# Moving head rows, chunk preparation and x1 statistics to other points of a step schedule

## The chip, the cores and the metric

One NeuronCore of a Trainium2 chip runs the whole program. The metric is the device time of one execution in microseconds. The five engines are called by the profile's names: PE is the matmul engine, DVE the vector engine, ACT the scalar engine, POOL the GpSimd engine, and SP the engine whose queue issues nearly all DMAs of the part that is changed.

## The reference

The input `r` is 8 sequences of 2048 points with 512 features. Two blocks follow each other, each with a layer norm in front, a layer norm behind, and a residual sum:

```python
def _L0_attn_ref(r, ...):                 # a state space layer
    ...
    h1 = jnp.fft.irfft(uf * Kf.T[None], n=nfft, axis=1)[:, :seq_len]
    y1 = h1 + D[0] * r
    return jax.nn.gelu(y1, approximate=False)

def _L0_ffn_ref(x, ...):                  # a gated recurrence over axis 0 (8 steps)
    def step(c, xt):
        ft = jax.nn.sigmoid(xt @ wf.T + c @ uf.T + bf)
        it = jax.nn.sigmoid(xt @ wi.T + c @ ui.T + bi)
        gt = jnp.tanh(xt @ wc.T + c @ uc.T + bc)
        return ft * c + it * gt, None
    c_final, _ = lax.scan(step, c0, x)
    return jnp.tanh(jnp.einsum('tbi,oi->tbo', x, wo) + c_final @ uo.T + bo)

x = L0_attn_r
x = x + _layernorm(_L0_attn_ref(_layernorm(x, axis=-1), ...), axis=-1)    # called x1 here
x = x + _layernorm(_L0_ffn_ref(_layernorm(x, axis=-1), ...), axis=-1)
```

The recurrence runs over the eight sequences: sequence index 0 to 7 is its time `t`, and each of the 2048 points is a row of its batch. So the output row of a point at any `t` needs the state after all eight steps.

## The kernel before, in words

**The first part** (up to about 690 us) computes the state space layer as a blocked convolution, group by group, and stores its result `y` to DRAM as `y_d`. Neither the diff nor anything in it touches this part.

**The second part** is the recurrence. The 2048 points are cut into four quarters `q` of 512 points, each of four chunks `cj` of 128. A step is one pair `(q, t)`; there are 32 steps, `n = 8 q + t`. The matrix products are done by a scheme with seven products in place of eight on 256-wide blocks, each in three fp16 pieces, so PE has many 128x256 matmuls (line 950).

A step is eight slots. Each holds one unit of PE's work: two units `z0`, `z1` (the output projection of x), and six gate units, called `g0` to `g5` here: input, candidate, forget gate for one half of the features, then the same for the other half. A unit is done in two pieces. `part_a` makes four products for a z unit and, for `t > 0`, eight for a gate unit; ACT (line 988) and DVE (lines 989 to 992) then add partial sums in PSUM. `part_b` makes the rest, and ACT evacuates: lines 1002 and 1003 (tile `zt`) for a z unit, line 1016 for a gate. The next unit's `part_a` lies between the two pieces of a unit. With `t > 0`, `part_b` of `z1` waits until after `part_a` of `g1`. PSUM has three `u` buffers for these units. The last gate of a half also makes the new state (`state`, lines 1036 to 1042) and its fp16 pieces `cf` (lines 1049 and 1051), which the next step's gates need.

**Points.** Everything else is hung on the points of this chain. Slot `s` has the points `2s` (after its `part_a`) and `2s + 1` (after the `part_b` that follows). A step therefore has the points 0 to 15, and 16 is point 0 of the next step. `put(functions, base, points)` appends one function to each point's list, and `go(p)` runs that list; a later `put` comes later in the list:

```python
put(turn(*steps[n + 1], i), b, ps[i])
...
part_a(key)
go(p)
...
finish(before, p + 1)        # part_b; the store of a z unit is put at its next point
go(p + 1)
```

In this part the order of PE, ACT, DVE, POOL and SP is the program's order. Each engine runs its own list in that order, so the first instruction that must wait holds up all behind it on its engine. What is hung on the points:

- `prep`: one chunk of x1 for two values of `t`: load `y` (SP, line 880), load `xr` (SP, 890), stat (DVE, 462 to 465), scale (POOL, 471 to 476), sum (ACT 903, POOL 904), store to `x1_d` (SP, 911; the DRAM tensor `x_d` in the profile). The tiles `y` and `xr` have one buffer each.
- `turn`: two chunks of x1 for the next step: load `xa` (SP, 925), stat, scale, norm (ACT, 936), split (PE transposes, 485, with ACT 489 and DVE 490 to 492), halves (`xf`: ACT 101 and DVE 102 in alternation). It runs twice in a step, `i = 0, 1`.
- `head`: one output row block of the quarter before (128 points at one `t`; 32 in a quarter, in the seven steps with `t > 0`: five in each of the first four, four in each of the last three). Load `zr` (SP, 1120; every eighth head also `ur`, 1118), sum (POOL, 1123), gate (ACT, 1126), stat, scale, load `x1r` (SP, 1136), out (ACT 1140, POOL 1141), store (SP, 1144). `zr` has four buffers, `x1r` two.
- `last`: in the step `t = 0` of a quarter, the part of the output that depends on the final state of the quarter before: four groups of 128x512 matmuls (450 to 452) in the same three `u` buffers, evacuated by ACT (1097) and summed by POOL (1100). It has a loaded `bo` in an `x1r` buffer, and its four `u_` tiles in `zr` buffers.
- the store of a z unit (SP, 1007 to 1009). The tile `zt` has one buffer: the next z unit's evacuation waits for that store.

After the last step comes `tail`: the 32 rows of the last quarter in 16 pairs. It loads `zz` (SP, 1157) and `xx` (SP, 1169), sums (DVE 1174), and stores (SP, 1190); the tiles are reused after nine pairs, so a later load of `xx` waits for an earlier pair's store.

Of the kernel before, what the change touches and what calls it, by code (L numbers as in the profile page):

```python
# [22 lines left out]
NB = 8  # L23
# [36 lines left out]
def s4_gated_block(ctx, tc, a, dbg=None):  # L60
# [54 lines left out]
    with ExitStack() as sctx:  # L115
        sp = sctx.enter_context(tc.tile_pool(name="setup", bufs=1, side="right"))
        ps = sctx.enter_context(tc.tile_pool(name="setup_ps", bufs=2, space=PSUM))
# [337 lines left out]
    def lnstat(src, tag):  # L455

        n = len(src)
        st = FE.tile([P, n, 6], F32, name="st" + tag)
        mv = FE.tile([P, n, 2], F32, name="mv" + tag, bufs=2)
        rs = FE.tile([P, n], F32, name="rs" + tag, bufs=2)  # L460
        for i, v in enumerate(src):
            V.bn_stats(st[:, i], v)  # L462
        for i in range(n):
            V.bn_aggr(mv[:, i], st[:, i])
        V.tensor_scalar(rs, mv[:, :, 1], EPS, None, ALU.add)  # L465
        return n, mv, rs, tag

    def lnscale(s_, neg=True):

        n, mv, rs, tag = s_  # L470
        Q.tensor_tensor(rs, rs, nhalf[:, 0:n], ALU.pow)  # L471
        mu = mv[:, :, 0]
        if neg:
            mu = FE.tile([P, n], F32, name="nm" + tag, bufs=2)
            Q.tensor_tensor(mu, mv[:, :, 0], rs, ALU.mult)
            Q.tensor_scalar(mu, mu, -1.0, None, ALU.mult)
        return [(mu[:, i : i + 1], rs[:, i : i + 1]) for i in range(n)]
# [102 lines left out]
    with ExitStack() as cctx:  # L580
# [220 lines left out]
        for g in range(NG):  # L801
# [17 lines left out]
            with tc.manual_schedule(engines=MAN if nxt else MAN | {mybir.EngineType.SP}):  # L819
# [18 lines left out]
                for s_ in range(NJ):  # L838
                    if s_ % 2 == 0 and s_:
                        conv_out(g, s_ // 2 - 1)  # L840
                    if nn:

                        d = ND1 if g == 1 else 0
# [71 lines left out]
    def turn(q, t, i):  # L915

        xa, s_ = [], []

        src = xa if q or t > 1 else [early["x1", i + 2 * h] for h in range(2)]

        def load():
            for h in range(2):
                x = FE.tile([P, H], F32, name="xa", bufs=2)
                if src is xa:
                    dma(out=x, in_=x1_d[QC * q + i + 2 * h, :, t])
                xa.append(x)

        def stat():
            s_.append(lnstat(src, "x"))

        def scale():
            s_.extend(lnscale(s_.pop()))

        def norm():
            for x, v, (nm, rs) in zip(xa, src, s_):
                S.activation(x, v, AF.Identity, scale=rs, bias=nm)

        def split_():
            pt = pq_.tile([P, 2, KT, P], F32, name="pt")
            xa[:] = [forms(q, t, i, xa, [pt[:, h] for h in range(2)])]  # L940

        return load, stat, scale, norm, split_, lambda: xa[0]()
# [168 lines left out]
    def head(q, cj, t):  # L1111

        c, s_ = QC * q + cj, {}

        def load():
            if c not in us_:
                us_[c] = FJ.tile([P, H], F32, name="ur", tag="wr")
                dma(out=us_[c], in_=u_d[c])
            s_["z"] = FT.tile([P, H], F32, name="zr", bufs=4)
            dma(out=s_["z"], in_=z_d[c, :, t])  # L1120

        def sum_():
            Q.tensor_tensor(s_["z"], s_["z"], us_[c], ALU.add)  # L1123

        def gate():
            S.activation(s_["z"], s_["z"], AF.Tanh, scale=1.0 / SW)

        def stat():
            s_["s"] = lnstat([s_["z"]], "h")

        def scale():
            s_["s"] = lnscale(s_["s"])[0]

        def load_x():
            s_["x"] = FT.tile([P, H], F32, name="x1r", bufs=2)
            dma(out=s_["x"], in_=x1_d[c, :, t])

        def out():
            nm, rs = s_["s"]
            S.activation(s_["z"], s_["z"], AF.Identity, scale=rs, bias=nm)  # L1140
            Q.tensor_tensor(s_["x"], s_["x"], s_["z"], ALU.add)  # L1141

        def store():
            dma(out=a["out"][c, :, t], in_=s_["x"])

        return load, sum_, gate, stat, scale, load_x, out, store
# [62 lines left out]
    def put(fs, base, ps):  # L1209
        for f, p in zip(fs, ps):  # L1210
            todo.setdefault(base + p, []).append(f)
# [5 lines left out]
    steps = [(q, t) for q in range(NQB) for t in range(NB)]  # L1217
    pairs = [(q, tp) for q in range(NQB) for tp in range(NB // 2)]
    chunks = [(g, cj) for g in range(1, len(pairs)) for cj in (0, 2, 1, 3)]
    at_ = lambda *p: [tuple(range(i, i + 6)) for i in p]  # L1220
    when = [(0, (0, 0, 3, 4, 5, 6)), (0, (0, 0, 5, 6, 7, 8)), (0, (9, 9, 11, 12, 13, 14))] + [(1, p) for p in at_(1, 6)]
    PA, PB = (5, 5, 7, 8, 10, 11), (12, 12, 16, 17, 19, 20)
    for n, (q, t) in enumerate(steps):

        if n > 1 and t:
            when += [(n, p) for p in (at_(5, 10, 15) if t in (2, 3) or n == 4 else at_(5, 10) if t == NB - 1 else (PA, PB))]
    end = last(NQB - 1)
    rows = [tail(NQB - 1, cj, tp, 4 * cj + tp) for cj in range(QC) for tp in range(NB // 2)]

# [5 lines left out]
    for n, (q, t) in enumerate(steps):  # L1235
        b = 16 * n
        if n + 1 < len(steps):
            ps = ((2, 5, 6, 7, 8, 9), (9, 10, 11, 12, 13, 14)) if n else ((0, 1, 2, 3, 5, 6), (5, 6, 7, 8, 9, 10))
            for i in range(2):
                put(turn(*steps[n + 1], i), b, ps[i])  # L1240
        if q and t == 0:
            put(last(q - 1), b, (-1, 4, 3, 5, 5, 7, 7, 9, 13, 14, 15))
        if n == len(steps) - 1:
            put(end[:2], b, (2, 3))
            for i in range(3):
                put(rows[i][:2], b, (8 + 2 * i, 9 + 2 * i))
        for (gp, cj), (n_, p) in zip(chunks, when):
            if n_ == n:
                put(prep(*pairs[gp], cj, (1, 0, 2)[cj] if n == 0 else 0), b, p)
        if q and t:  # L1250
            for i in range(5 if t < 5 else 4):
                r = 5 * t - 5 + i - max(t - 5, 0)
                put(head(q - 1, r // NB, r % NB), b, [1 + 3 * i + d for d in (0, 2, 4, 6, 8, 9, 10, 12)])
    with tc.manual_schedule(engines=MAN | {mybir.EngineType.SP}):
        before = None
        for n, (q, t) in enumerate(steps):
# [8 lines left out]
            for sl, key in enumerate(zs + gs if n else gs[:5] + zs + gs[5:]):  # L1265
                p = 16 * n + 2 * sl
# [85 lines left out]
```

## Time and profile before

| | us |
|---|---|
| median of 3 runs (2898.7 to 2905.06) | 2899.93 |
| the profiled execution's own time | 2900.85 |
| its span | 2899.1 |
| PE busy | 2588.2 (89%) |
| DVE busy | 2102.1 (73%) |
| ACT busy | 1478.8 (51%) |
| POOL busy | 1185.9 (41%) |
| DMA, mean | 156 GB/s |

The times of the profile count from the start of the span. The profiled execution is 1.75 us longer than its span and 0.92 us longer than the median. In the timeline a line gives start, duration, engine, source line, operation, tiles and count; the bracket behind it is the idle time of that engine before it, and what ended it. "SPq" is SP's queue of DMA issues.

### The profile page before, as it was taken

The page shows a single profiled execution, that of the slowest core. Times are in us where ns is not written, and L with a number is a line of the kernel's source. Part 1 is how long each engine was busy: PE and PEld are TensorE (multiplying, and loading weights), DVE is VectorE, ACT ScalarE, POOL GpSimd, SP SyncE. Part 2 cuts the span into 40 slices and gives each one's busy share as a digit, 9 for nine tenths or more (in the row PEclk, how much of TensorE's full clock was granted, in tenths as well). Part 3 has the DMA queues.
Part 4 walks back from the last instruction along what each step waited for, and adds up shares of the span by engine and source line. Part 5 has one row for each costly group of instructions (what it writes and reads, how often), then busy time and mean ns, then how long its engine had stood idle before and what let it go on. Part 6 is the DMA issues. An engine that isn't in the chain of part 4 may idle for free.

```text
span 2899.1 us, 60027 instructions
## 1 busy us (share of the span) xinstructions
PE 2588.2 (89%) x23940; PEld 2255.6 (78%) x23940; DVE 2102.1 (73%) x4248; ACT 1478.8 (51%) x3091; POOL 1185.9 (41%) x1496
## 2 busy tenths in 40 slices
PE   4678888885999999999999998999999899999990
PEld 3367777774888888878888886888888788888870
DVE  7868877747666776667777776777777677777757
ACT  8956666643434443445555454454545445444435
POOL 5757667714112221114454341345443324443227
PEclk8789999987999999999999999999999999999995
DMA  6867878787423433324664443355554334532338
GB/s 233 304 209 241 259 251 260 241 248 189 154 66 95 114 84 96 91 88 124 160 172 135 121 124 99 101 159 167 145 149 120 117 89 147 151 117 89 95 119 298
DMA packets 521937, 451.10 MB, mean 156 GB/s; under 512 B 289974, under 2 KB 401080, under 8 KB 516664
## 3 DMA queue, kind: packets, MB, share of 16 engines
q1 hardware_dynamic: 521224, 446.74, 52.0%
q8 instruction: 187, 3.06, 0.4%
q14 instruction: 94, 0.77, 0.1%
q10 hardware_dynamic: 432, 0.52, 0.1%
HBM read 295.41 MB, written 151.78 MB: 154 GB/s over the span
## 4 chain that ended last, share of the span: by engine, by line
PE 50%; DVE 13%; ACT 5%; DMA 4%; issue 2%; POOL 1%; SPq 0%; POOLq 0%; DVEq 0%; ACTq 0%
PE u L950 47%; PE pt L485 1%; DVE u L992 1%; DMA z_d<-zc 1%; DVE cf L1051 1%; ACT xf L101 1%; DVE cd L1037 1%; DMA y<-y_d 1%; ACT gate L1016 1%; DVE sty L462 1%; DVE gate L1036 1%; ACT y L903 1%; DMA z_d<-zt 1%; DVE u2p L989 1%; DVE sth L462 1%
## 5 line engine op out<-in xcount | busy, mean ns | idle before, releaser
L950 PEld LDWEIGHTS <-w 128*128 128x128 f16 x15120 | 1482.0, 98 | 216.0 <-issue 30.8
L950 PE MATMUL u<-xf,w 128*128 128x256 f16 x8064 | 945.4, 274 | 32.1 <-ACT zt L1003 15.4
L950 PE MATMUL u<-cf,w 128*128 128x256 f16 x7056 | 825.9, 273 | 1.5 <-DVE cf L1051 1.5
L950 PE MATMUL u<-w,xf 128*128 128x256 f16 x2688 | 314.2, 275 | 15.2 <-DVE u L992 5.2
L1141 POOL TENSOR_TENSOR x1r<-x1r,zr 128x512 f32<-128x512 f32 x96 | 133.6, 1392 | 453.8 <-ACT zr L1140 344.6
L988 ACT ACTIVATE u2p<-u 128x256 f32<-128x256 f32 x256 | 96.7, 378 | 433.9 <-PE u L950 433.7
L1016 ACT ACTIVATE gate<-u,bias 128x512 f32<-128x512 f32 (+1 forms) x384 | 200.6, 574 | 217.9 <-PE u L950 217.8
L904 POOL TENSOR_TENSOR xr<-y,xr 128x512 f32<-128x512 f32 x120 | 160.1, 1354 | 351.7 <-ACT y L903 351.5
L950 PEld LDWEIGHTS <-xf 128*128 128x128 f16 x2688 | 264.6, 99 | 49.8 <-issue 10.7
L989 DVE TENSOR_TENSOR u2p<-u2p,u 128x256 f32<-128x256 f32 x256 | 106.8, 417 | 258.7 <-ACT u2p L988 256.8
L992 DVE TENSOR_TENSOR u<-u,u2p 128x512 f32<-128x512 f32 x256 | 179.0, 699 | 8.8
L647 POOL TENSOR_TENSOR u<-xg,u 128x512 f16<-128x512 f32 x104 | 128.7, 1242 | 124.6 <-ACT u L645 124.6
L641 POOL TENSOR_TENSOR xg<-xg,mu 128x512 f32<-128x512 f32 x112 | 162.7, 1459 | 9.7 <-DMA xg<-in_xr 9.7
L471 POOL TENSOR_TENSOR rsy<-rsy,nhalf 128x2 f32<-128x2 f32 (+1 forms) x68 | 49.4, 726 | 284.3 <-DVE rsy L465 272.4
L102 DVE TENSOR_TENSOR x<-pxt,x 128x256 f16<-128x256 f32 x240 | 100.1, 418 | 70.7 <-ACT x L101 69.5
L1021 DVE SCALAR_TENSOR_TENSOR gate<-gate,gate 128x1024 f32<-128x1024 f32 x64 | 88.2, 1378 | 83.2 <-ACT gate L1016 82.8
L462 DVE BATCH_NORM_STATS2 sty<-y 128x6 f32<-128x512 f32 x120 | 76.8, 682 | 86.9 <-DMA y<-y_d 86.9
L1123 POOL TENSOR_TENSOR zr<-zr,ur 128x512 f32<-128x512 f32 x96 | 125.7, 1309 | 20.9 <-DMA zr<-z_d 16.4
L101 ACT ACTIVATE x<-pxt 128x256 f16<-128x256 f32 x240 | 91.2, 381 | 79.6 <-PE pxt L667 73.4
L452 PE MATMUL pyt<-u,t 128*128 128x128 f16 (+2 forms) x544 | 124.8, 229 | 5.5 <-POOL u L623 5.5
L450 PE MATMUL pyt<-u,t 128*128 128x128 f16 (+2 forms) x544 | 121.8, 224 | 6.2 <-ACT y L746 3.1
L101 ACT ACTIVATE xf<-pt 128x512 f16<-128x512 f32 x124 | 60.7, 490 | 128.6 <-DVE xf L102 116.5
(371 smaller groups left out, 5352.2 us busy)
## 6 DMA issues: line engine op xcount, KB each, us to landing
xs<-in_rr SPq DMA_DIRECT2D x32, 1024.0 KB, 7.1
t<-kpad SPq DMA_DIRECT2D x32, 1024.0 KB, 5.5
y_d<-y SPq DMA_DIRECT2D x30, 1024.0 KB, 7.5
xr<-in_r SPq DMA_DIRECT2D x60, 512.0 KB, 5.6
xa<-x_d SPq DMA_DIRECT2D x120, 256.0 KB, 4.1
y<-y_d SPq DMA_DIRECT2D x59, 512.0 KB, 5.8
x_d<-xr SPq DMA_DIRECT2D x59, 512.0 KB, 3.2
xg<-in_xr SPq DMA_DIRECT2D x28, 1024.0 KB, 8.3
```

The lines of the kernel that those rows point to most:

```text
L101: S.activation(hi, src, AF.Copy)
L452: T.matmul(out, lhsT=w(0), rhs=x(1), start=False, stop=stop)
L462: V.bn_stats(st[:, i], v)
L641: Q.tensor_tensor(xg, xg, bc(mu1), ALU.subtract)
L647: (V if g == 2 else Q).tensor_tensor(u[:, js, 1], xg, u[:, js, 0], ALU.subtract)
L904: Q.tensor_tensor(xv, yv, xv, ALU.add)
L950: T.matmul(u[:, d], lhsT=w(f, b, i == 1, k), rhs=x(f, b, i == 2, k), start=opens and bank not in seen, stop=stop and j == len(n) - 1, skip ...
L989: V.tensor_tensor(u2, u2, u[:, UY], ALU.add)
L992: V.tensor_tensor(u[:, 2:4], u[:, 2:4], u2[:, None].to_broadcast([P, 2, BP]), ALU.add)
L1016: act = lambda o, s_, b: S.activation(o, s_, AF.Tanh, scale=gsc[kind], bias=b)
L1123: Q.tensor_tensor(s_["z"], s_["z"], us_[c], ALU.add)
L1141: Q.tensor_tensor(s_["x"], s_["x"], s_["z"], ALU.add)
```

## The change

Nothing is computed differently, and no instruction is added or taken away; functions are put at other points.

```diff
-    at_ = lambda *p: [tuple(range(i, i + 6)) for i in p]
-    when = [(0, (0, 0, 3, 4, 5, 6)), (0, (0, 0, 5, 6, 7, 8)), (0, (9, 9, 11, 12, 13, 14))] + [(1, p) for p in at_(1, 6)]
-    PA, PB = (5, 5, 7, 8, 10, 11), (12, 12, 16, 17, 19, 20)
+    two = (2, 2, 5, 6, 7, 8), (8, 8, 10, 11, 12, 13)
+    three = (-2, -2, 4, 5, 6, 7), (6, 7, 9, 9, 10, 11), (10, 11, 15, 16, 17, 18)
+    when = [(0, (0, 0, 3, 4, 5, 6)), (0, (0, 0, 5, 6, 7, 8)), (0, (9, 9, 11, 12, 13, 14))] + [(1, p) for p in two]
     for n, (q, t) in enumerate(steps):
 
         if n > 1 and t:
-            when += [(n, p) for p in (at_(5, 10, 15) if t in (2, 3) or n == 4 else at_(5, 10) if t == NB - 1 else (PA, PB))]
+            when += [(n, p) for p in (three if t in (2, 4) or n == 6 else two)]
...
-            ps = ((2, 5, 6, 7, 8, 9), (9, 10, 11, 12, 13, 14)) if n else ((0, 1, 2, 3, 5, 6), (5, 6, 7, 8, 9, 10))
+            ps = ((2, 5, 6, 7, 8, 9), (9, 10, 11, 12, 13, 14)) if t else ((2, 4, 5, 6, 7, 8), (7, 8, 9, 10, 11, 13)) if n else ((0, 1, 2, 3, 5, 6), (5, 6, 7, 8, 9, 10))
...
         if q and t:
             for i in range(5 if t < 5 else 4):
                 r = 5 * t - 5 + i - max(t - 5, 0)
-                put(head(q - 1, r // NB, r % NB), b, [1 + 3 * i + d for d in (0, 2, 4, 6, 8, 9, 10, 12)])
+                put(head(q - 1, r // NB, r % NB), b, [2 * i + d for d in (0, 2, 3, 5, 6, 5, 7, 8)])
```

The points of a `prep` stand in the order load, load_x, stat, scale, sum, store; of a `turn` load, stat, scale, norm, split, halves; of a `head` load, sum, gate, stat, scale, load_x, out, store. So a head started every three points and lived for twelve; it starts every two and lives for eight. The last store of a step's heads moves from point 25 (five heads) or 22 (four) to 16 or 14. `prep` no longer reaches past point 13, but for the third of the steps with three, which ends at 18; those are the steps `t = 2, 4` (and `t = 6` in the first quarter), where they were `t = 2, 3` (and 4 in the first). `turn` moves in the steps `t = 0` of the last three quarters alone.

## The prediction

> **What bounds the kernel now.** The page first. PE is busy nearly the whole span, so what can be won is PE's idle time, and the chain behind the last matmul.
>
> ```profile
> PE 2588.2 (89%) x23940; PEld 2255.6 (78%) x23940; DVE 2102.1 (73%) x4248; ACT 1478.8 (51%) x3091; POOL 1185.9 (41%) x1496
> ```
>
> Next, stretches of the second part: a step without heads, then the starts of the second and third quarters (steps t = 0), then a step with heads (t = 3, last quarter). Columns: stretch, length, busy time and count of PE, PEld, DVE, ACT, POOL, the granted clock, DMA.
>
> ```profile
> 1142.00:1208.00 66.00, 66.00 (x607) 59.34 (x606) 44.75 (x88) 28.79 (x59) 15.72 (x21) 1.00 0.30 81
> 1208.00:1270.00 62.00, 54.02 (x411) 40.64 (x409) 40.62 (x79) 27.13 (x57) 8.98 (x11) 0.97 0.26 86
> 1732.00:1799.00 67.00, 57.50 (x430) 42.58 (x429) 40.37 (x79) 30.23 (x61) 16.33 (x20) 0.95 0.28 91
> 2468.00:2536.00 68.00, 64.57 (x590) 57.58 (x588) 51.94 (x107) 33.84 (x66) 33.20 (x46) 1.00 0.60 159
> ```
>
> A step without heads is PE alone: 66 us, no idle time, 66/607 = 0.109 us a matmul. A step with heads idles 3.4 us, a quarter's start 8.0 or 9.5. Third, what PE waited for between 1200 and 2810 us (in total, times, longest):
>
> ```profile
> PE u L950 <- ACT zt L1003: 15.4, 19, 2.2
> PE u L450 <- ACT zt L1003: 7.9, 3, 3.6
> PE u L451 <- DVE cf L1051: 4.9, 5, 2.2
> PE pt L485 <- ACT xa L936: 3.5, 3, 1.2
> PE u L950 <- ACT u__16431 L1097: 3.0, 1, 3.0
> ```
>
> With its other lines it sums to 50.2 us. Placed by the timeline's brackets, 17.4 us in 22 waits lie in the first third of steps t >= 2 and 33.0 us in the three quarter starts (7.8, 12.5, 12.7). A wait costs 0.16 us more than its bracket, since a matmul takes 0.273 us and the next starts after 0.109.
>
> Fourth, the timeline behind such a wait (q = 1, t = 4; the step starts at 1463.3):
>
> ```profile
> 1479.85 0.80 ACT L1140 ACTIVATE zr<-zr,nmh,rsh 128x512 f32<-128x512 f32 x1
> 1480.55 0.61 ACT L1126 ACTIVATE zr<-zr 128x512 f32<-128x512 f32 x1
> 1482.24 2.78 PE L950 MATMUL u<-xf,w 128*128 128x256 f16 x24 [0.86 <-ACT zt L1003]
> 1487.51 0.32 SPq L911 DMA_DIRECT2D x_d<-xr  x1
> 1489.66 0.38 SPq L1007 DMA_DIRECT2D z_d<-zt  x1
> 1494.22 0.38 ACT L1002 ACTIVATE zt<-u 128x256 f32<-128x256 f32 x1 [4.58 <-DMA z_d<-zt]
> 1495.15 2.78 PE L950 MATMUL u<-xf,w 128*128 128x256 f16 x24 [1.61 <-ACT zt L1003]
> ```
>
> Two ACT instructions of heads stand between the `cf` pieces and `zt` of z0, and PE loses 0.86. Then z0's store stands in SP's queue behind a chunk's store, which waited for POOL; the second `zt` waits for that store, and PE for `zt`. At a quarter's start the same happens, worse (1749 to 1757): a head's store, bo's load behind it, and z0's store only at 1752.19.
>
> Last, the end of step t = 0 (1263) and the tail:
>
> ```profile
> 1261.88 0.38 ACT L101 ACTIVATE xf<-pt 128x256 f16<-128x256 f32 x1 [2.23 <-DVE xf L102]
> 1263.11 0.59 ACT L1097 ACTIVATE u__16431<-u 128x512 f32<-128x512 f32 x1
> 1263.75 4.41 PE L950 MATMUL u<-w,xf 128*128 128x256 f16 x24 [3.04 <-ACT u__16431 L1097]
> 2823.44 0.34 SPq L1144 DMA_DIRECT2D out<-x1r  x1
> 2823.87 0.38 SPq L1157 DMA_DIRECT2D zz<-z_d  x1
> 2845.42 0.32 SPq L1169 DMA_DIRECT2D xx<-x_d  x1
> ```
>
> The halves of turn 1 (point 14) hold ACT while DVE is at its `u2p` chain; `u_` comes after them, and PE lacks its buffer. In the tail SP stands before the last head's store until 2823.44; the pairs' loads come after it.
>
> **Part 1, starts of steps, about 15 us gained.** The 22 waits cost 17.4 + 22 x 0.16 = 20.9 us. A head now ends at point 16, so between points 0 and 2 neither ACT nor DVE has head work; ACT gets 1.41 us (0.80 + 0.61) back ahead of `zt`, more than the 0.86 lost, and the 0.85 and 0.35 to 0.41 waits for DVE and `cf` go with the head and chunk statistics (0.68 to 1.9 us each) leaving the edge. z0's store then goes out when `zt` is written, some 14 us into the step, and lands 4.1 us later (median of that DMA); the second `zt` is due at 23.6 (24 + 36 + 24 + 18 + 48 + 48 + 18 matmuls x 0.109).
>
> The exception is the step after one with three chunks (t = 3 and 5, six times). The third chunk's store is at point 2, followed there by the loads of the next chunk, and `xr` has one buffer: its load waits for that store to land. By the rows: `cf` done at 13 us into the step, `y` on ACT to 14.6 (1.51), POOL sum to 16.5 (2.5), store, landing 3.2 after issue, so `xr` near 20, two head loads, z0's store at 21.4, landed near 26. The second `zt` ends near 27.3, PE wants the buffer at 27.5. The step's second head queues behind the same load: its `zr` lands at 24.6, and ACT's gate waits for it and POOL's sum, to the same 26. So between 0 and 3.5 us each; I take 1, six times 6 us. 20.9 - 6 = 15. In the first quarter (no heads; steps 3, 5, 7 now follow three chunks) PE shows no wait between 760 and 1208; bound 0 to 3 us, I take 0.
>
> **Part 2, edge of quarters, about 15 us.** At the second quarter's start, where no heads precede it, the waits up to the second `zt` are 0.34 + 1.01; at the third 2.21 + 0.34 + 0.16 + 3.28, at the fourth 0.42 + 1.63 + 0.34 + 0.16 + 3.63. The new heads end at point 14 there, so both become like the first: 4.6 and 4.8 us of waits, 0.8 us of their 0.16s, and the half clock behind the long ones: after 3.28, eighteen 512-wide matmuls at 0.43 instead of 0.215 for most of their run, 3.1 us by the starts; 1.7 at the fourth. Sum 15.
>
> **Part 3, turn in t = 0, about 4 us, of both signs.** Slots here are short (24 and 18 matmuls). Turn 1's halves go from point 14 to 13, where 18 matmuls of `last` and a `part_a` (6.5 us) cover them: the 3.04 goes, with 1.8 us of half clock in two of three cases, and the 1.17 for `xa`, as the norm is two points earlier. But turn 0's halves go from 9 to 8, in front of g1's evacuation. Queued behind them on ACT is line 1016, and the `part_a` of g3 waits for it. Step by step: ACT `u2p` 0.38 after g2's end, `xf` 0.59, DVE's chain of four (2.06) and its 0.68, ACT 0.38 + 1.05, then gate 0.50 + 1.05: 6.0 us after g2's `part_a`, where PE is free after 1.97. A wait of 4.0 in place of 1.14, and half clock behind it, 0 to 3.1, I take 1.8. The 1.14 before `last`'s third group falls to 0.45, covered by the transposes (0.87) now ahead of it. Before, with the 0.16s: 3 x 7.1 + 3.6 = 25.0. After: 3 x (0.45 + 0.2 + 4.0 + 0.48 + 1.8) = 20.8. If the cover at point 13 fails, 12 us are lost instead.
>
> [...]
>
> **Part 4, tail, about 5 us.** The last two heads' stores (2818.22, 2823.44) leave SP; they went out after the last matmul. The loads of pairs 3 to 8 went out from 2823.9 to 2833.9 and the first pair's store, in that crowd, took 10 us to free `xx` (2835.23 to 2845.42); each later load waits 5.7 to 6.2 us for the next store, down to 2875.3. Earlier loads let that store land in the usual 5.6 and leave at 2833.9. That is 5 to 6 us earlier through the chain; DVE, which waits there (2.73, 1.71, 3.76), would follow. Bounds 0 and 7.
>
> **What costs nothing.** Per head: four SP DMAs, POOL 1.27 + 1.0 + 1.27, ACT 0.62 + 0.80, DVE 1.0, all moved, none new. In mid-step a gate's slot is 9.2 us of PE and its chain needs 2.5, so 6.7 us of delay on ACT and DVE together is covered; the densest point (7: norm 1.51, `y` 1.51, out 0.80, gate 0.62) makes 4.4. `zr` is reused by the fourth next head, whose load (point 8) follows the out at 7. `x1r`'s load waits for a store one point before, landing in 2.6 us (median), while a point is 4. Behind it wait prep's and turn's loads; turn 1's `xa` would issue at 40 us into the step, land at 44, and DVE reaches it near 46.5.
>
> **Sum.** 15 + 15 + 4 + 5 = 39 us. 2900.85 - 39 = 2861.9 for the profiled execution, which stood 0.9 above the median; I predict 2862.
>
> **Rivals.**
> *A. The new landing wait decides.* `xr`'s wait for the chunk store puts z0's store later than counted, at the upper bound of 3.5 us in six steps (-15). Alone that leaves 24 us, 2877. With part 3 at a worse end (half clock of 3.1 us after all three waits: -4; the cover at point 13 failing: -12) and a tail that gives nothing (-5, as DMA moves 257 GB/s there already) it leaves 7 to 15, about 2889. For it: SP shows 354 us of waiting at that chunk store. Against: a wait of SP costs only what stands behind it.
> *B. Slower.* SP's queue clogs at points 8 and 9: chunk store, its landing, head store, its landing, and behind them turn 1's `xa`. DVE, in order, stands before `xa`'s statistics and holds the gates' `u2p` chain. DVE covers about 6 us there; beyond it every step with heads pays, 21 of them. From 39/21 = 1.9 us a step it eats the gain; at 3 us, 63 - 39 = +24, 2924. For it: the store's longest landing is 7.4 us. Against: 2.6 is the median.
> *C. Nothing*: the waits only change names, 2896 to 2904.
>
> **How the numbers follow.** Forecast (gains of 25 to 55) 0.60, A (gains of 7 to 25) 0.21, B 0.13, C 0.06. A measurement can tell 0.2%, about 5.8 us, so the forecast and A make faster 0.81, C same 0.06, B slower 0.13. The range goes from 2848 (the 6 us of part 1 not paid, and 8 of part 3's new wait hidden) to 2888 (through nearly all of A); B and C stay outside.
>
> **What would show it.** Right: waits of PE for `zt` in the matmuls of line 950 fall from 15.4 to below 7, and sit in steps t = 3 and 5; the 3.04 for line 1097 is gone; a wait for line 1016 of about 4 us appears in each t = 0; the tail's first `xx` reload is 5 us sooner after the last matmul. Wrong: new PE waits in mid-step, or DVE waiting for `xa<-x_d` in every step.

## The result, and the profile after

The changed kernel takes 3007.62 us (median of 4 runs, 3001.71 to 3011.18) against 2899.31 us for the kernel before beside it. The ratio is 1.0374, with an interval of 1.0354 to 1.0394: slower by 108 us, where 39 us of gain were forecast. The execution in its profile took 3006.43 us, its span 3004.6 us, so 105.5 us more than the span before.

The first view of the page, busy time by engine, answers to the first line shown of before:

```profile
PE 2621.0 (87%) x23940; PEld 2264.2 (75%) x23940; DVE 2118.7 (71%) x4248; ACT 1481.1 (49%) x3091; POOL 1176.5 (39%) x1496
```

The counts are the same. PE is busy 32.8 us longer for the same matmuls, so part of the loss is a lower clock (the mean granted clock is 0.957, 0.962 before), and the rest is idle time.

What PE waited for between 1200 and 2920 us (in total, times, longest):

```profile
PE u L950 <- DVE u L992: 63.1, 32, 3.9
PE u L950 <- ACT zt L1003: 17.1, 5, 4.4
PE u L950 <- ACT gate L1016: 16.6, 12, 3.9
PE pt L485 <- ACT xa L936: 14.9, 5, 4.4
...
PE u L450 <- ACT zt L1003: 3.0, 3, 1.0
PE u L950 <- DVE cf L1051: 3.0, 8, 0.9
```

The line on top is new: before, the wait for DVE's line 992 was one of 0.8 us. With all its lines this window's sum rises from 54.4 us in 48 waits to 123.7 in 74; between 705 and 1200 us it rises from 17.7 in 7 to 24.4 in 13. The last matmul starts at 2942.49 instead of 2829.69, 112.8 us later. Of that, 76.0 are these waits, and about 5 the 0.16 us that each of the 32 added waits costs beyond its bracket. The remaining 32 are put down to the lower clock behind the waits; the 32.8 us that PE is busy longer agree with it. From the last matmul to the end of the span it is 62.1 us instead of 69.4: the tail gives 7.3 back.

Line 992 is the end of DVE's partial sums of a unit. What made it late is in the groups of the page, which show what ended the idle time just before each group:

```profile
L490 DVE TENSOR_TENSOR ts<-pt,b 128x512 f32<-128x512 f32 x62 | 42.6, 687 | 237.7 <-ACT b L489 229.6
...
L1123 POOL TENSOR_TENSOR zr<-zr,ur 128x512 f32<-128x512 f32 x96 | 127.4, 1328 | 207.3 <-DMA zr<-z_d 202.7
...
L489 ACT ACTIVATE b<-pt 128x256 f32<-128x256 f32 x124 | 40.5, 380 | 261.3 <-DMA z_d<-zc 250.1
```

ACT, in order, stood 250 us in front of line 489 until a DMA out of `zc` had landed, and DVE behind it 230 us. Among ACT's waits between 1200 and 2920 us it is the largest:

```profile
ACT b L489 <- DMA z_d<-zc: 202.1, 20, 12.5
```

Before, the same wait was 39.7 us in 13, 5.5 at the longest, all of it in this window.

Line 489 belongs to `turn`'s split and has nothing to do with `zc`, but for the buffer. In the code the two tiles are declared with one tag, of one buffer:

```python
b1 = FJ.tile([P, 2, 2, P], F32, name="b1", tag="un")        # line 486, in turn's split
...
gates["z"] = FJ.tile([P, 2, BP], F32, name="zc", tag="un")  # line 980, the z units
```

`zc` is free when the store of `z1`, the second z unit of the step, has landed (line 1009). The timeline of one step (q = 1, t = 1, from point 7 on) follows it through:

```profile
1304.68 0.38 ACT L988 ACTIVATE u2p<-u 128x256 f32<-128x256 f32 x1 [0.15 <-PE u L950]
...
1305.21 0.32 SPq L911 DMA_DIRECT2D x_d<-xr  x1
1305.63 0.53 SPq L880 DMA_DIRECT2D y<-y_d  x1
1308.49 1.29 SPq L890 DMA_DIRECT2D xr<-in_r  x1
1309.88 0.42 SPq L1144 DMA_DIRECT2D out<-x1r  x1
1310.39 0.38 SPq L1120 DMA_DIRECT2D zr<-z_d  x1
1310.82 1.13 SPq L1007 DMA_DIRECT2D z_d<-zt  x1
...
1312.53 0.45 SPq L1009 DMA_DIRECT2D z_d<-zc  x1
...
1316.84 0.66 ACT L489 ACTIVATE b<-pt 128x256 f32<-128x256 f32 x2 [11.78 <-DMA z_d<-zc]
1317.53 0.69 DVE L490 TENSOR_TENSOR ts<-pt,b 128x512 f32<-128x512 f32 x1 [10.38 <-ACT b L489]
...
1326.60 2.14 PE L950 MATMUL u<-xf,w 128*128 128x256 f16 x18 [2.31 <-DVE u L992]
...
1339.06 3.79 PE L950 MATMUL u<-xf,w 128*128 128x256 f16 x18 [2.01 <-DVE u L992]
```

At point 8 SP's list is: the first chunk's store, the second chunk's `y` and `xr` loads, a head's store, a head's load, and only then `z1`'s store. `z1`'s last piece of `zt` was written at 1296.43, so its store was ready to go nearly 9 us before the chunk's store, on which SP stood for 16.3 us until POOL had the chunk's sum. The chunk's store goes out at 1305.21, just when ACT comes to line 489; `xr` has one buffer, so its load stands until that store has landed, at 1308.49. `z1`'s store leaves between 1310.82 and 1312.53 and lands at 1316.84, and ACT has stood still for 11.78 us. Behind line 489 on ACT are the evacuations of a gate (1016) and the halves, on DVE the split and two gates' `u2p` chains; by 1326.60 and again at 1339.06 PE has nothing left to run. With `z1`'s store put in front and nothing else moved (`z1_first` below), ACT stands 0.49 us in front of line 489 in this step, and PE has no wait in it.

### The profile page after: what moved, and what is told of

Its sections match the earlier page's. It is cut to its first block, busy times and chain, and to the rows that moved or that the text cites. A ratio compares the mean times of both kernels' runs of the same rounds, so it can differ in the third digit from the quotient of the medians.

```text
span 3004.6 us, 59995 instructions
## 1 busy us (share of the span) xinstructions
PE 2621.0 (87%) x23940; PEld 2264.2 (75%) x23940; DVE 2118.7 (71%) x4248; ACT 1481.1 (49%) x3091; POOL 1176.5 (39%) x1496
## 3 DMA queue, kind: packets, MB, share of 16 engines
q8 instruction: 187, 3.06, 0.4%
## 4 chain that ended last, share of the span: by engine, by line
PE 32%; DVE 21%; DMA 8%; ACT 5%; POOL 3%; issue 3%; SPq 3%; ACTq 0%; POOLq 0%; DVEq 0%
PE u L950 30%; DMA z_d<-zc 3%; DMA x_d<-xr 3%; POOL xr L904 2%; DVE cf L1051 2%; DVE cd L1037 2%; DVE gate L1036 2%; DVE xf L102 2%; ACT gate L1016 1%; ACT xf L101 1%; DVE u L992 1%; SPq L890 1%; DVE gate L1021 1%; DVE sth L462 1%; ACT xa L936 1%
## 5 line engine op out<-in xcount | busy, mean ns | idle before, releaser
L950 PE MATMUL u<-xf,w 128*128 128x256 f16 x8064 | 969.1, 278 | 116.5 <-DVE u L992 74.0
L1141 POOL TENSOR_TENSOR x1r<-x1r,zr 128x512 f32<-128x512 f32 x96 | 139.7, 1455 | 346.8 <-ACT zr L1140 341.7
L490 DVE TENSOR_TENSOR ts<-pt,b 128x512 f32<-128x512 f32 x62 | 42.6, 687 | 237.7 <-ACT b L489 229.6
L471 POOL TENSOR_TENSOR rsx<-rsx,nhalf 128x2 f32<-128x2 f32 (+1 forms) x66 | 55.2, 836 | 352.5 <-DVE rsx L465 352.5
L489 ACT ACTIVATE b<-pt 128x256 f32<-128x256 f32 x124 | 40.5, 380 | 261.3 <-DMA z_d<-zc 250.1
L452 PE MATMUL pyt<-u,t 128*128 128x128 f16 (+2 forms) x544 | 124.7, 229 | 5.0 <-POOL u L623 5.0
```

Of the source, the lines that this page charges most:

```text
L452: T.matmul(out, lhsT=w(0), rhs=x(1), start=False, stop=stop)
L950: T.matmul(u[:, d], lhsT=w(f, b, i == 1, k), rhs=x(f, b, i == 2, k), start=opens and bank not in seen, stop=stop and j == len(n) - 1, skip ...
```

## The experiments

Theory S, the store: the new `prep` points put a chunk's store, its landing and a load ahead of `z1`'s store, so that `zc`, and with it line 489, comes free too late. Its narrow form says that the landing wait of the second chunk's `xr` does it. Rival H, the heads: two points apart they crowd ACT, DVE and POOL. Short diffs are against the kernel before ("before +") or the changed one ("after +"); "..." stands for code left out. The kernel before ran beside each; its median lay between 2896.8 and 2900.5 us, so versions are compared by their ratio to it.

### Which of the three parts

`heads_only`: before + the new points of the heads.

```diff
-                put(head(q - 1, r // NB, r % NB), b, [1 + 3 * i + d for d in (0, 2, 4, 6, 8, 9, 10, 12)])
+                put(head(q - 1, r // NB, r % NB), b, [2 * i + d for d in (0, 2, 3, 5, 6, 5, 7, 8)])
```

> The kernel before with the new head points alone. Theory S (the store of z1, which frees the tile that zc and b1 share, stands too far back in SP's queue, and what puts it back is the chunk store and the load that waits for its landing, both new at point 8): the heads add only one store and one load ahead of it, and their work leaves the edges, so this is faster than before by 10 to 25 us, about 2880, and ACT waits for z_d<-zc under 60 us in total. Rival H (two x1r buffers at two-point spacing clog SP by themselves): slower by at least half of the 108 us, 2950 or more, with SP waiting for out<-x1r about 69 us as in the changed kernel.

Measured: 2895.68 us, 0.9985 (0.9976 to 0.9994), a gain of about 4 us. PE's waits, then ACT's:

```profile
PE u L950 <- DVE u L992: 18.1, 6, 3.4
...
PE u L950 <- ACT zt L1003: 2.4, 3, 1.9
```

```profile
ACT b L489 <- DMA z_d<-zc: 89.5, 20, 7.2
```

The starts of steps get what was forecast (15.4 us of waits for `zt` fall to 2.4), and the wait for `zc` takes it away again. H is out as the cause of the loss, since it expected 2950 or more. But S missed too: the gain is below the 10 to 25 us that it expected, and the wait for `zc` above its 60. With the new heads alone `z1`'s store is late too; `heads_turn_z` below shows what that was worth.

`prep_only`: before + the new `two`, `three` and `when`, heads and turn as before.

> The kernel before with the new chunk points alone. Theory S: slower by 50 to 110 us (2950 to 3010), since the chunk store, then a load that waits for its landing, stand ahead of z1's store at point 8; ACT waits for z_d<-zc over 150 us. Rival H: within 20 us of before.

Measured: 3054.93 us, 1.0534 (1.0519 to 1.0548): 155 us slower, beyond the range expected. PE waits 56.4 us in 33 for DVE's line 992, ACT 150.7 us for `zc`. The chunk points alone make the loss and more. Not all of it goes through `zc`: PE's waits for `zt` rise as well, to 32.7 us in 22, and those for `xa` to 24.1 in 8.

`turn_only`: before + the new `ps`.

> The kernel before with the new x1 points of the steps t = 0 alone. Both theories: a wait of about 3.9 us of PE for line 1016 in three places and the 3.04 us for line 1097 gone; by the prediction's part 3 a gain of about 4 us (2 to 8), since in the changed kernel the half clock behind the new wait is not seen everywhere.

Measured: 2891.48 us, 0.9963 (0.9949 to 0.9977), 11 us gained, more than expected. Heads and turn without the new chunk points (`heads_turn`, before + both):

> The kernel before with the new head points and the new turn points of t = 0, chunks as before. If the parts add: 2900 - 4.5 - 10 = 2886 (2880 to 2891).

Measured: 2883.10 us, 0.9948 (0.9936 to 0.9961). 0.0015 and 0.0037 add up to it: 15 us. Beside the new chunk points the same two are worth 0.0534 - 0.0374 = 0.016, 46 us, so the parts don't add: the new chunk points cost more beside the old heads than beside the new ones. Why was not traced.

### Which wait it is

`z1_first`: after + the store of `z1` first in its point's list.

```diff
-                if st_:
+                if st_ and key[2:] == ("z", 1):
+                    todo.setdefault(p + 1, []).insert(0, st_)
+                elif st_:
```

> The changed kernel, with the store of z1 put at the front of the list of its point 8 and not at its end; nothing else moves. Theory S: ACT's wait for z_d<-zc falls from 250 us to under 60 and 70 to 110 us come back, 2895 to 2935; the waits for zt in the steps t = 3 and 5 stay. Rival H: less than 30 us come back, 2975 or more, as heads and chunk loads stand as they did.

Measured: 2925.72 us, 1.0080 (1.0064 to 1.0096). One DMA group, ahead of the others at its point, brings back 0.0294, 85 of the 108 us. The wait for `zc` and PE's for line 992:

```profile
ACT b L489 <- DMA z_d<-zc: 50.5, 5, 11.0
```

```profile
PE u L950 <- DVE u L992: 13.3, 5, 3.5
```

Over the whole span ACT's wait for `zc` falls from 250.1 to 67.1 us, a little above the 60 expected; the five waits shown sit in steps with three chunks. For 85 of the 108 us S is shown. `two_gap` asks for the narrow form. After +:

```diff
-    two = (2, 2, 5, 6, 7, 8), (8, 8, 10, 11, 12, 13)
+    two = (2, 2, 5, 6, 7, 8), (9, 9, 11, 12, 13, 14)
```

> The changed kernel with the second chunk of a step with two a point later, (9, 9, 11, 12, 13, 14): at point 8 SP still has the first chunk's store ahead of z1's store, but no longer the load that waits for its landing. Theory S in its narrow form (the landing wait is what costs): ACT's waits of 12 us for z_d<-zc become 7 to 8 in these steps, and 40 to 75 us come back, 2930 to 2965. If the chunk store's own wait for POOL is what costs: under 25 us come back, 2980 or more.

Measured: 2944.63 us, 1.0162 (1.0146 to 1.0178): 0.0212, 61 us back. The second chunk's loads now stand behind `z1`'s store, not before it; the whole second chunk is a point later too, so the edit isn't the wait alone. In the steps with two chunks ACT's waits become 3.4 to 7.6 us, where they were 10.5 to 12.4; in the step shown 7.61, from 11.78. These 4.2 us are what the two loads took of SP there, 1305.63 to 1309.78: about 2.2 of them the landing wait, the rest the issue of the two loads. So over half of the loss goes with the two loads in front of `z1`'s store, but the narrow form, that it is the landing wait alone, is not shown. By the rows of this step, what `two_gap` leaves of the 85 is the other DMAs ahead of the store, its own issue and landing, which come too late once it stands behind the chunk's store, and the steps with three chunks, which this edit leaves as they are.

`z_first`: after + both z stores first (`key[2] == "z"`).

> The changed kernel with the stores of z0 (point 4) and of z1 (point 8) at the front of their points' lists. Theory S: with z1's store alone in front, 2925.7 us were left, with PE still waiting 17.6 us for zt and 18.2 for xa, in the steps t = 3 and 5; these come from z0's store behind the load that waits for a chunk store's landing, at point 2, which moving it within point 4 passes only past a head's load. So if the loss is at point 2, little comes back, 2915 to 2930; if the head's load at point 4 were the cause, 2890 to 2905.

Measured: 2912.90 us, 1.0051 (1.0036 to 1.0067): 8 us more, just under the range. Most of what is left sits in steps around three chunks (q = 1, t = 3):

```profile
1417.27 0.33 SPq L911 DMA_DIRECT2D x_d<-xr  x1
...
1421.97 2.23 SPq L890 DMA_DIRECT2D xr<-in_r  x1
1424.25 0.46 SPq L1120 DMA_DIRECT2D zr<-z_d  x1
...
1429.96 0.63 ACT L1126 ACTIVATE zr<-zr 128x512 f32<-128x512 f32 x1 [10.55 <-POOL zr L1123]
```

The third chunk's store at point 2, its landing, `xr`, and behind them a head's `zr` load; ACT stands at that head's gate for 10.55 us, and the z unit's evacuation is behind it. `z0`'s store is in front here, and PE still waits 14.5 us for `zt`, against 17.6 in `z1_first`: this route does not go through that store.

### The change without its chunk points

`heads_turn_z`: before + heads, turn, and both z stores first.

> The same with both z stores at the front of their points' lists. Theory S: what the new heads still lose, ACT's waits for z_d<-zc (89.5 us in 20 waits, longest 7.2) and PE's 18 us for line 992, goes: 2862 to 2878, faster than either. Rival (spacing of the heads by itself costs): no better than the one without, 2882 or more.

Measured: 2862.28 us, 0.9876 (0.9861 to 0.9891), 0.0072 or 21 us under `heads_turn`. ACT's wait for `zc` falls to 14.4 us, PE's for line 992 to 11.1, not to nothing. That it is the forecast time of the changed kernel is chance; it is another kernel. The stores alone, `before_z` (before + both z stores first):

> The kernel before with nothing but the z stores at the front of their points' lists. Theory S: PE's waits for zt (15.4 + 7.9 us) fall by about half, since part of them are ACT's own order and not the store; 2880 to 2892. If the stores' place in the queue matters only with the new points: 2895 to 2902.

Measured: 2877.93 us, 0.9933 (0.9921 to 0.9946), 19 us, slightly more than expected. The kernel before had paid for the same order in small, and mostly by the other tile of the store: between 1200 and 2920 us ACT's 64.6 us for the store of `zt` fall to 1.6, its 39.7 for `zc` to 19.1.

`best`: `heads_turn_z` with the halves of turn 0 in `t = 0` left at point 9 (the diff is against `heads_turn_z`).

```diff
-            ps = ... ((2, 4, 5, 6, 7, 8), (7, 8, 9, 10, 11, 13)) if n else ...
+            ps = ... ((2, 4, 5, 6, 7, 9), (7, 8, 9, 10, 11, 13)) if n else ...
```

> New head points, z stores at the front of their points' lists, chunks as before, and the new turn points of t = 0 with turn 0's halves left at point 9. Theory: the three waits of 3.9 us for line 1016 shrink to about 1.1 (3 x 2.8 = 8 us) with the half clock behind them where there was one, so 2848 to 2856 against 2862 with the halves at point 8. If the halves have another cover to lose, 2860 to 2866.

Measured: 2852.94 us, 0.9848 (0.9834 to 0.9861), the fastest version: 44 us under the kernel before. PE's waits for line 1016, first of `heads_turn_z`, then of `best`:

```profile
PE u L950 <- ACT gate L1016: 11.7, 3, 3.9
```

```profile
PE u L950 <- ACT gate L1016: 3.4, 3, 1.1
```

### Whether the chunk points can be mended

`chunks_clear`: after + both z stores first, and every chunk load kept off the points at which a z store or a gate's head load would stand behind it.

```diff
+    two = (5, 5, 7, 8, 9, 10), (10, 10, 12, 13, 14, 15)
+    three = (0, 0, 4, 5, 6, 7), (8, 8, 10, 10, 11, 12), (12, 12, 15, 16, 17, 18)
+    one = (1, 2, 3, 4, 5, 6), (6, 7, 8, 9, 10, 11)
...
```

`one` is used in step 1 in place of `two`.

> The changed kernel with the z stores in front and the chunks' points moved so that no load that waits for a chunk store's landing stands between a head's load at points 0 to 4 and its use, nor at point 7 ahead of z1's store: two = (5, 5, 7, 8, 9, 10), (10, 10, 12, 13, 14, 15), three = (0, 0, 4, 5, 6, 7), (8, 8, 10, 10, 11, 12), (12, 12, 15, 16, 17, 18), step 1 as before. If the landing waits are the whole of what the new chunk points cost: 2860 to 2880, against 2913 with the z stores in front alone. If something else of the chunks costs (DVE or POOL too dense in mid-step): 2895 or more.

Measured: 2878.32 us, 0.9936 (0.9921 to 0.9951), near the upper end. `clear_2`: the same, but in `three` the second and third chunk as in the changed kernel, `(6, 7, 9, 9, 10, 11), (10, 11, 15, 16, 17, 18)`.

> As chunks_clear, but the steps with three chunks keep the second and third chunk of the changed kernel, (6, 7, 9, 9, 10, 11), (10, 11, 15, 16, 17, 18): the landing wait at point 7 is back, the one at point 2 stays away. With z stores in front alone PE waited 14.5 us for zt (point 2, five times), and 21.5 for xa and 6.7 for line 992 (point 7). By these shares: zt's waits gone, xa's still there, 2888 to 2900. If point 2 was the whole: 2875 to 2882, as chunks_clear.

Measured: 2901.91 us, 1.0015 (1.0004 to 1.0026). That is just over the 2888 to 2900 expected, and it refutes that point 2 was the whole remainder: the points 7 and 11 of the three-chunk steps cost 0.0079, 23 us. The share expected for `xa` was wrong: PE's waits for it are 14.6 us here and 16.0 in `chunks_clear`. What differs is the same route again, in eleven waits, against 9.1 and 22.8 us in `chunks_clear`:

```profile
PE u L950 <- DVE u L992: 24.2, 11, 3.8
```

```profile
ACT b L489 <- DMA z_d<-zc: 58.8, 10, 11.2
```

The steps one after another; 0.0001 of the ratio is 0.29 us:

| kernel | ratio | step |
|---|---|---|
| changed kernel | 1.0374 | |
| `z1`'s store first | 1.0080 | 85 us |
| `z0`'s store first too | 1.0051 | 8 us |
| loads off point 2, and `two` off point 8 (`clear_2`) | 1.0015 | 10 us |
| loads of `three` off the points 7 and 11 (`chunks_clear`) | 0.9936 | 23 us |
| the old chunk points (`heads_turn_z`) | 0.9876 | 17 us |
| halves of turn 0 back at 9 (`best`) | 0.9848 | 8 us |

**What stays open.** The 17 us between `chunks_clear` and `heads_turn_z`. In the first PE still waits for the norm of a turn, five times in the steps with three chunks:

```profile
PE pt L485 <- ACT xa L936: 16.0, 5, 5.4
```

`heads_turn_z` has no such wait among its listed ones. Whether SP's queue or the amount of work on DVE and POOL in these steps makes it was not separated. A buffer of its own for `zc`, the direct test of the shared tag, was not tried either.

## Why the prediction was wrong

**The step that failed: "What costs nothing".** It listed what a head moves, and found 6.7 us of cover against 4.4 us of added delay on ACT and DVE. The chunks' new points were so put at nothing beyond part 1's 6 us; alone they cost 155 us (`prep_only`). Two things were not in that list. First, the `two` points were not walked through SP's queue for the sum: the landing wait of `xr` was worked out for the third chunk at point 2 alone, in part 1, though the second chunk's load at point 8 stands behind the first chunk's store at point 8 in the same way, in most steps. Second, `z1`'s store, which is behind all of it, was left out; that it frees the buffer of `b1`, which the split at the same point wants, could be read in two tags, and in a line of the waits of before, small as it is:

```profile
ACT b L489 <- DMA z_d<-zc: 39.7, 13, 5.5
```

A delay of ACT of 12 us is then nearly twice the cover. The sign that the prediction named for being wrong, new PE waits in mid-step, is the line on top of PE's waits after. The paragraph also had `x1r`'s load find its store landed; SP stands 68.9 us in 37 waits for it between 1200 and 2920, though the new heads without the chunk points still gain 4 us.

**Rival B** named the place, SP's queue at points 8 and 9 with the store, its landing and a head's store, and got 0.13. Its victim was wrong: DVE waited for `xa` 5.5 us in 4 in the whole kernel, ACT 250.1 for `zc`. Its price was too: it set 3 us a step as the bad case; in the step shown above it is 2.31 + 2.01 = 4.3 us and a lower clock behind the second (18 matmuls in 3.79 us, 2.14 behind the first), and `z1_first` puts 85 us on it. **Rival A's** mechanism, the landing wait, is part of the cause (of the 61 us that go with the two loads), but it was counted for `z0`'s store in six steps, not for `z1`'s in most.

**Part 1, starts of steps.** Of the 22 small waits the 17 for `zt` are gone, and PE's remaining waits for `zt` in line 950 are five, in t = 3 and 5 as said: 3.58, 3.02, 3.03, 3.06 and 4.44 us. I took 1 of a bound of 0 to 3.5, so the term was mis-sized. Of the two routes it named, the second pays: at the first of the five the head's `zr` load behind the landing holds ACT for 11.0 us. The first does not show: ACT's wait for the store of `zt` is 0.6 us in all between 1200 and 2920. The waits for `cf` in line 950, which were to go, rise from 1.5 us in 4 to 3.0 in 8. The first quarter, taken at 0, shows 6.7 us of added waits.

**Part 2, edge of quarters.** Right for `zt`: PE's waits for it in line 450 fall from 7.9 to 3.0 us, 1.0 at each start; the waits of 3.28 and 3.63 are gone, and the lower clock behind them: there twelve 128x512 matmuls (the prediction has eighteen) took 5.08 and 4.08 us by the starts, at a granted clock of 0.50 and 0.63, and now take 2.6 us. A wait of 1.59 us for `cf` stays at the third and the fourth quarter's start (2.21 and 1.63 before), which the sum took away. So by these rows the part is worth nearer 12 us than 15.

**Part 3, turn in t = 0.** Right in each detail that could be read. At the second quarter (the bracket of the first line is the wait for `last`'s third group, predicted 0.45; the last line is the new wait, predicted 4.0 with 1.8 of half clock):

```profile
1240.99 0.38 PE L450 MATMUL u<-uw,cf 128*128 128x512 f16 x1 [0.37 <-ACT gate L1016]
...
1244.87 4.75 PE L950 MATMUL u<-xf,w 128*128 128x256 f16 x42
1253.51 6.41 PE L950 MATMUL u<-xf,w 128*128 128x256 f16 x42 [3.89 <-ACT gate L1016]
```

42 matmuls take 6.41 us behind the wait, at a granted clock of 0.73, and 4.75 ahead of it: 1.66 us. It is 6.41 behind the other two such waits as well (1830.48, 2410.63), so the clock was paid all three times, where the expectation of `turn_only` has it not seen everywhere. What the sum took for the two old waits, 1.8 us each, was somewhat large: 24 matmuls behind them took 4.41 and 4.13 us, and 2.78 at full clock. The waits for lines 1097 and 936 in t = 0 are gone. Alone the edit was worth 11 us and not 4; where the other 7 or so lie was not traced. `best` shows that turn 0's halves are better left at 9; turn 1's at 13 were not run alone.

**Part 4, tail.** Right, and a little small: 7.3 us against 5, just over the upper bound of 7. The first reload of `xx` starts 7.6 us after the last matmul, 15.7 before.

## What to carry to other kernels

Before moving a DMA in an in-order queue, write down the queue's list at the new point, and for each store behind it ask which buffer it frees and who takes that buffer next, by tag and not by the tile's name. Here a store that had to wait for its data (16.3 us of SP in the step shown) and a load that had to wait for that store's landing (2.2 us) held up everything behind them in the queue, so a store that is ready and frees a single buffer belongs in front of both. A small wait in the profile of before between two things that have nothing to do with each other (here 39.7 us of ACT for `zc`) can mark a shared buffer, and is the first place to look at when the order around it changes.

## What the runs showed of the hardware

PE's clock can fall behind waits shorter than the 3.04 us of the prediction's rows. In the changed kernel ten waits for line 992 last 2.00 or 2.01 us; behind seven of them the next 18 matmuls take 2.12 or 2.14 us, behind the other three 2.94, 3.79 and 3.79 (and 3.03 for the 18 after the 2.94). The stretches behind one of the three and one of the seven, in the columns of the stretches shown before (the granted clock is the third number from the right):

```profile
1339.10:1343.00 3.90, 3.90 (x21) 2.79 (x21) 3.87 (x6) 0.90 (x2) 1.26 (x1) 0.56 0.56 157
1639.95:1644.00 4.05, 4.05 (x38) 3.63 (x38) 4.01 (x6) 0.93 (x2) 1.26 (x1) 1.00 0.33 104
```

The same wait costs 1.7 us more or nothing. On the other side, a wait of 3.58 us (at 1450.13) was followed by 24 matmuls in 2.78 us, full speed. The three waits of 3.04 us of the kernel before were followed by 24 matmuls in 4.41, 2.78 and 4.13 us (at 1263.75, 1802.47 and 2338.66, with a granted clock of 0.61, 1.00 and 0.66), and in the changed kernel waits of 3.02, 3.03 and 3.06 us by 24 in 2.78, 4.33 and 2.78. The three waits of 3.89 us were all paid. So between 2.0 and 3.6 us the length of a wait does not tell in these runs whether it is paid, and what decides it was not shown. For a sum this means that also a wait of 2 us carries an uncertain 0 to 1.7 us. Of the ten, three paid it, some 5 us of the 32 put down to the clock; the rest came behind other waits, most of them longer, such as the three of 3.89 us and six for line 992 of 2.31 to 3.01 us, behind which 18 matmuls took 2.80 to 3.75 us.
